# Graph network, layers 2 and 3: the vector and scalar engines follow one order written by hand instead of the scheduler's, and the edge bias is worked out in layer 1

## Chip, cores and metric

The kernel runs on one core of a Trainium2 chip. The metric is the device time of one execution in microseconds. Six engines appear in the profile: PE (matrix multiply) with PEld (its weight loads), DVE (vector), ACT (scalar), POOL (GpSimd) and SP (sync). In this kernel SP starts the plain DMA transfers, and POOL starts the indirect ones, the gathers and scatters by index.

## What is computed

Four graph layers follow one another on 3125 nodes with 128 features and 100,000 edges. Each layer's result is added to its input and normalized. Layer 0 is an attention with relation types, layer 1 a mean over neighbours with two matrix products, layer 2 an attention with 4 heads, layer 3 an attention with one head and a key matrix for each of 8 edge types. The change is in layers 2 and 3, and in a corner of layer 1:

```
# layer 2
Q, K, V = (x @ Wq, x @ Wk, x @ Wv)                  # 4 heads of 32
edge_bias = edge_attr @ We
attn = jnp.sum(Q[dst] * K[src], axis=-1) * SCALE + edge_bias
attn = jnp.where(attn >= 0, attn, 0.2 * attn)
attn_exp = jnp.exp(attn - jnp.max(attn))
attn_sum = jax.ops.segment_sum(attn_exp, dst, num_segments=n)
attn_norm = attn_exp / jnp.maximum(attn_sum[dst], 1e-12)
agg = jax.ops.segment_sum(V[src] * attn_norm[:, :, None], dst, num_segments=n)
h = jnp.concatenate([x, agg @ Wo + bo], axis=1) @ Wm + bm
return jax.nn.relu(h)

# layer 3
Q, K, V = (_type_matmul(x, W_Q, node_type), ...)
k_t = _type_matmul(K[src], W_edge, edge_type)
scores = jnp.sum(Q[dst] * k_t, axis=-1) / scale * mu[edge_type]
attn = _sparse_softmax(scores, dst, N)
out = jax.ops.segment_sum(V[src] * attn[:, None], dst, num_segments=N)
```

## The kernel before

The nodes are sorted by degree and cut into 25 tiles of 128, one node in each partition. `CAP[t]` is the number of edge slots that tile t has for each of its nodes: 57, 42, 40 and so on down to 21, together 821. Slots are handled in chunks of `W` = 8, so tile t has CAP[t]/8 chunks, rounded up; over all tiles there are 114. What exceeds the slots is taken by a loop (`behind`) that makes no trip with these inputs.

Layers 2 and 3 have the same shape. For each slot POOL issues one gather (`gather`, L103): 128 rows of 256 floats, keys in the first half and values in the second, from a table in DRAM (`kv_tab` in layer 2, `ktv_tab` in layer 3) into a chunk buffer `kv`. There are 8 such buffers in layer 2 and 12 in layer 3. A chunk then passes four long DVE instructions:

- `qk<-kv,qp` (L1220 in layer 2, L1378 in layer 3) multiplies the keys with the query of the node,
- `lg<-qk` (L1221, L1379) adds that up to one logit for each slot and head,
- `msg<-kv,ex` (L726, in `weigh`) multiplies the values with the softmax weights,
- `u<-msg` (L730) adds the weighted values over the slots, and `accb<-accb,u` (L731) adds `u` to the sum of the tile.

Between the second and the third stands a chain of short instructions for each group of chunks (in layer 2 a group is up to 3 chunks, from `segments`; in layer 3 all chunks of a tile): edge bias and leaky step in layer 2 (`biased`, L1226 to L1232), then in `weights` the maximum (L701), the new maximum `mn` (L703), `corr` (L705), the subtraction (L706), the exponentials on ACT (L707, L708), and the totals (L711 to L715). A tile in layer 2 ends with `closing` (matrix products on PE, a layer norm) and `table3`, which works out the tile's rows of `ktv_tab` on PE and ACT and has POOL scatter them (`put`, L106); a tile in layer 3 ends with a layer norm and a scatter of the output.

No order is written out: a scheduler places the instructions of all engines, and adds the semaphores. A buffer comes free when the last instruction that reads it is done; a gather into it waits for that on POOL, and everything behind it in POOL's queue waits too. In layer 2 the index of a gather comes from `pay_sb`, a 2463 KB array that SP loads at the start of layer 2 (L1201); it also holds the edge attributes of the bias.

Of the kernel before, what the change touches and what calls it, by code (L numbers as in the profile page):

```python
# [8 lines left out]
F32 = mybir.dt.float32  # L9
F16 = mybir.dt.float16  # L10
BF16 = mybir.dt.bfloat16
I32 = mybir.dt.int32
# [76 lines left out]
def tile_gnn(ctx, tc, a, out):  # L89
# [633 lines left out]
    def weigh(pool, acc, val, ex, n, heads):  # L723

        msg = pool.tile([P, W, D], F32, name="msg")
        V.tensor_tensor(msg[:, :n, :].rearrange("p s (h d) -> p s h d", h=heads),  # L726
                        val.rearrange("p s (h d) -> p s h d", h=heads),
                        ex.unsqueeze(3).to_broadcast([P, n, heads, D // heads]), op=OP.mult)
        u = pool.tile([P, D], F32, name="u", bufs=1)
        V.tensor_reduce(u, msg[:, :n, :].rearrange("p s d -> p d s"), AX.X, OP.add)  # L730
        V.tensor_add(acc, acc, u)  # L731

    def query(ps, q):

        qp = ps.tile([P, D], F32, name="qp", bufs=2)
        A.activation(qp, q, AF.Copy)
        return qp

# [329 lines left out]

    with ExitStack() as ctx1, tc.tile_pool(name="l1", bufs=2) as wp, tc.tile_pool(name="l1s", bufs=1) as sp:
# [90 lines left out]
        nc.sync.dma_start(xn, x1_tab.rearrange("(t p) d -> p t d", p=P))  # L1160
        for c in range(NCW):
# [30 lines left out]
    early.close()  # L1192


    H2 = 4
# [4 lines left out]
    pay_sb = big.tile([P, NS, PW], I32, name="pay_sb")  # L1200
    nc.sync.dma_start(pay_sb.rearrange("p s w -> p (s w)"), pay_tab)  # L1201
    with tc.tile_pool(name="l2", bufs=2) as wp, tc.tile_pool(name="l2s", bufs=1) as sp, \
            tc.tile_pool(name="l2p", bufs=1, space=PSUM) as ps1:

        we = row_of(sp, a["L2_gnn_We"].rearrange("k h -> (k h)"), 3 * H2, "we")
        weT = we.rearrange("p (k h) -> p h k", k=3)
        m = sp.tile([P, NT, H2], F32, name="m")
        V.memset(m, LOW)
# [6 lines left out]
        def rows2(qp, pl, n, lg):  # L1215
            kv = wp.tile([P, W, 2 * D], F32, name="kv", bufs=8)
            for s in range(n):
                gather(kv[:, s, :], kv_tab, pl[:, s, 0:1])
            qk = wp.tile([P, W, D], F32, name="qk")
            V.tensor_mul(qk[:, :n], kv[:, :n, :D], qp.unsqueeze(1).to_broadcast([P, n, D]))  # L1220
            V.tensor_reduce(lg, qk[:, :n].rearrange("p s (h d) -> p s h d", h=H2), AX.X, OP.add)  # L1221
            return kv

        def biased(pl, n, lg, mk):
            eb = wp.tile([P, 5 * W, H2, 3], F32, name="eb")
            V.tensor_tensor(eb[:, :n], pl.bitcast(F32)[:, :, 3:6].unsqueeze(2).to_broadcast([P, n, H2, 3]),  # L1226
                            weT.unsqueeze(1).to_broadcast([P, n, H2, 3]), op=OP.mult)
            bias = wp.tile([P, max(CAP), H2], F32, name="bias")
            V.tensor_reduce(bias[:, :n], eb[:, :n], AX.X, OP.add)
            V.scalar_tensor_tensor(lg, lg, (D // H2) ** -0.5, bias[:, :n], op0=OP.mult, op1=OP.add)  # L1230
            V.scalar_tensor_tensor(lg, lg, 0.2, lg, op0=OP.mult, op1=OP.max)
            V.tensor_add(lg, lg, mk.unsqueeze(2).to_broadcast([P, n, H2]))  # L1232

        def behind2(t, pl, mk, rl):
            lg = wp.tile([P, max(CAP), H2], F32, name="lg")
            kv = rows2(query(ps1, qb[:, t, :]), pl, W, lg[:, :W])
            biased(pl, W, lg[:, :W], mk)
            ex = ps1.tile([P, max(CAP), H2], F32, name="ex")
            corr = softmax(wp, lg[:, :W], W, H2, m[:, t, :], l[:, t, :], ex[:, :W])
            faded(accb[:, t, :], corr, H2)  # L1240
            weigh(wp, accb[:, t, :], kv[:, :, D:], ex[:, :W], W, H2)
# [21 lines left out]
        def closing(t, scale):  # L1263
# [13 lines left out]
            T.matmul(h_ps, oT, wm[:, 1, :], start=False, stop=True)  # L1277
            y = wp.tile([P, D], F32, name="y")
            V.tensor_add(y, h_ps, bm)
            V.scalar_tensor_tensor(y, y, 0.0, xb[:, t, :], op0=OP.max, op1=OP.add)  # L1280
            layernorm(wp, xb[:, t, :], y, t)

        def table3(t):


            of = wp.tile([P, NTY, P], F32, name="of", bufs=1)
            for k in range(NTY):
                V.tensor_scalar(of[:, k, :], ident, is_t[:, k, t:t + 1], None, op0=OP.mult)
            xk_ps = ps1.tile([P, NTY, P], F32, name="xk_ps", tag="dense")
            T.matmul(xk_ps, xb[:, t, :], of, start=True, stop=True)  # L1290
            xkT = wp.tile([P, NTY, P], F32, name="xkT", bufs=1)
            A.activation(xkT, xk_ps, AF.Copy)
            p_ps = ps1.tile([P, 3 * D], F32, name="p_ps")
            for k in range(NTY):
                T.matmul(p_ps, xkT[:, k, :], wqkv[:, k, :], start=(k == 0), stop=(k == NTY - 1))
            qkv = wp.tile([P, 3 * D], F32, name="qkv")
            A.activation(qkv, p_ps, AF.Copy)
            V.tensor_copy(qb[:, t, :], qkv[:, :D])
            kT = transposed(wp, ps1, qkv[:, D:2 * D], "kT")
            rows = wp.tile([P, NET, 2 * D], F32, name="rows")  # L1300
            for e0 in range(0, NET, 4):
                e_ps = ps1.tile([P, 4, D], F32, name="e_ps", bufs=2)
                T.matmul(e_ps, kT, wed[:, e0:e0 + 4, :], start=True, stop=True)
                V.tensor_mul(rows[:, e0:e0 + 4, :D], e_ps, mu[:, e0:e0 + 4].unsqueeze(2).to_broadcast([P, 4, D]))
            A.activation(rows[:, :, D:], qkv[:, 2 * D:].unsqueeze(1).to_broadcast([P, NET, D]), AF.Copy)
            put(ktv_tab, od, t, rows.rearrange("p e f -> p (e f)"))

        for t in range(NT):
            qp = query(ps1, qb[:, t, :])
            for s0, s1, run in segments(t):  # L1310
                lg = wp.tile([P, max(CAP), H2], F32, name="lg")
                parts = []
                for c0, w in run:
                    o = OFF[t] + c0
                    parts.append(rows2(qp, pay_sb[:, o:o + w], w, lg[:, c0 - s0:c0 - s0 + w]))
                n, o = s1 - s0, OFF[t] + s0
                biased(pay_sb[:, o:o + n], n, lg[:, :n], mask[:, o:o + n])
                ex = ps1.tile([P, max(CAP), H2], F32, name="ex")
                corr, rest = weights(wp, lg[:, :n], n, H2, m[:, t, :], l[:, t, :], ex[:, :n])
                faded(accb[:, t, :], corr, H2)  # L1320
                for (c0, w), kv in zip(run, parts):
                    weigh(wp, accb[:, t, :], kv[:, :w, D:], ex[:, c0 - s0:c0 - s0 + w], w, H2)
                rest()

            rl = wp.tile([P, H2], F32, name="rl")
            V.tensor_scalar(rl, l[:, t, :], 1e-12, None, op0=OP.max)
            V.reciprocal(rl, rl)
            closing(t, rl)
            table3(t)
# [111 lines left out]
```

## Time and profile before

| | us |
|---|---|
| median of 3 runs | 5285.81 (5254.62 to 5292.59) |
| profiled execution, its own time | 5243.0 |
| profiled execution, span from first to last instruction | 5241.3 |
| layer 0 and setup, to 2490 | 2490 |
| layer 1, to 2668 | 178 |
| gather of the tiles' own rows (25 gathers), to 2707 | 39 |
| layer 2, first to last kv gather, to 3928 | 1221 |
| from there to the first gather of layer 3, to 4010 | 82 |
| layer 3, first to last gather, to 5192 | 1182 |
| to the end | 49 |

The profile is of one execution. "busy" of an engine is the time in which it executes; "idle before" is the time just ahead of an instruction in which its engine did nothing, with what ended it. "issue" there means that the profile shows nothing that it waited for, and "remote" (in the chain: "another core or an unknown queue") that a semaphore event did whose source the profile doesn't know. For POOL, a gather's busy time is the time of its issue; the data lands later.

### The profile page before, as it was taken

To read this page: it belongs to the slowest core of one execution; us is meant where nothing else is said; L and a number is where in the kernel's file an instruction comes from. 1 tells how busy PE (TensorE), PEld (TensorE's weight loads), DVE (VectorE), ACT (ScalarE), POOL (GpSimd) and SP (SyncE) were. 2 spreads that over 40 slices of the span, in tenths; PEclk is the share of its full clock that TensorE was granted. 3 is DMA by queue.
4 is the path that set the end of the run, shared out by engine and by line. 5 is a ranking of instruction groups with operands and counts; after the bars stand their busy time and mean duration, and the time that the engine had idled before them with its cause. 6 is when DMAs were issued, how large, how long until landed. Compare 5 with 4: busy or idle time off the path is not lost. (4 is left out here: it accounts for less than half of the span.)

```text
span 5241.3 us, 41048 instructions
## 1 busy us (share of the span) xinstructions
PE 2170.7 (41%) x12091; PEld 1405.0 (27%) x12091; DVE 3025.1 (58%) x7369; ACT 1018.4 (19%) x2777; POOL 2860.7 (55%) x3030
## 2 busy tenths in 40 slices
PE   7267676677767677777830122222232000000000
PEld 5145444455545454545310001011111000000000
DVE  8346555666656666656224576556664554454646
ACT  1023233333333333332100111111111000000000
POOL 0545444555545454453047666666663777666664
PEclk9578778778877787878865555555566555555555
DMA  3423222333323233332533333333342333233232
GB/s 82 122 80 86 80 80 80 87 99 90 99 79 87 75 90 86 82 97 75 215 106 99 99 109 106 109 105 113 104 113 73 105 96 93 79 92 94 86 92 58
DMA packets 213060, 498.45 MB, mean 95 GB/s; under 512 B 62329, under 2 KB 109100, under 8 KB 208185
## 3 DMA queue, kind: packets, MB, share of 16 engines
q0 software_dynamic: 136448, 397.65, 26.8%
q1 hardware_dynamic: 76344, 97.76, 6.0%
q8 instruction: 102, 1.67, 0.1%
q14 instruction: 166, 1.36, 0.1%
HBM read 424.65 MB, written 70.63 MB: 94 GB/s over the span
## 5 line engine op out<-in xcount | busy, mean ns | idle before, releaser
L103 POOL DMA_INDIRECT kv<-kv_tab,pay_sb x821 | 783.2, 954 | 384.9 <-issue 245.6
L103 POOL DMA_INDIRECT hs<-h_tab,srcx x821 | 848.3, 1033 | 262.0 <-issue 212.9
L103 POOL DMA_INDIRECT kv<-ktv_tab,pay_sb x821 | 802.6, 978 | 333.0 <-issue 244.2
L730 DVE TENSOR_REDUCE u<-msg 128x128 f32<-128x1024 f32 (+4 forms) x228 | 384.0, 1684 | 144.4 <-remote 94.6
L892 PE MATMUL zps<-oh,zq 128*128 128x512 bf16 x1232 | 397.4, 443 | 37.1 <-DVE oh L883 20.7
L835 PE MATMUL lg<-yw,low 128*128 128x8 f32 x1642 | 242.0, 274 | 150.0 <-ACT low L831 72.7
L849 POOL COPY hs<-gates 1x8 f32<-1x8 f32 (+3 forms) x133 | 41.2, 310 | 467.0 <-ACT gates L833 446.6
L835 PEld LDWEIGHTS lg<-yw,low 128*128 128x128 f32 x1642 | 234.5, 218 | 210.3 <-ACT low L831 100.1
L103 POOL DMA_INDIRECT zs<-z_tab,rel x205 | 213.1, 1039 | 124.7 <-issue 55.2
L623 ACT ACTIVATE c_oha<-c_oha,srclo 128x50 bf16<-128x50 bf16 (+2 forms) x821 | 206.0, 345 | 264.9 <-DVE c_oha L571 193.0
L904 PE MATMUL t_ps<-zw,zT 128*128 128x136 f32 x1232 | 225.7, 312 | 75.2 <-DVE hs L905 36.4
L905 DVE TENSOR_TENSOR hs<-hs,t_ps 128x408 f32<-128x408 f32 (+1 forms) x231 | 122.0, 528 | 227.8 <-PE t_ps L904 81.3
L726 DVE TENSOR_TENSOR msg<-kv,ex 128x1024 f32<-128x1024 f32 (+4 forms) x228 | 248.7, 1102 | 2.9 <-issue 1.8
L896 PE MATMUL pre<-zT,zw 128*128 128x512 f32 x308 | 205.7, 756 | 101.6 <-issue 62.4
L741 PE MATMUL tp<-ident,an 128*128 128x128 f32 x25 | 11.3, 453 | 560.7 <-DMA kv<-kv_tab,pay_sb 172.0
L904 PEld LDWEIGHTS t_ps<-zw,zT 128*128 128x128 f32 x1232 | 194.5, 213 | 109.7 <-issue 50.0
L898 PEld LDWEIGHTS pre<-ident,hs 128*128 128x128 f32 x1232 | 189.0, 221 | 95.3 <-issue 94.6
L824 PE MATMUL pre<-identb,hq 128*128 128x512 bf16 (+3 forms) x645 | 204.6, 417 | 5.9 <-issue 3.4
L831 ACT ACTIVATE low<-pre 128x512 f32<-128x512 f32 (+2 forms) x215 | 122.9, 574 | 400.8 <-PE pre L898 159.1
L1290 PE MATMUL xk_ps<-of,xqb 128*128 128x512 f32 x50 | 50.9, 1121 | 358.0 <-DVE xqb L759 204.9
L898 PE MATMUL pre<-ident,hs 128*128 128x128 f32 x1232 | 194.1, 306 | 0.0
L1378 DVE TENSOR_TENSOR qk<-kv,qp 128x1024 f32<-128x1024 f32 (+4 forms) x114 | 126.5, 1110 | 114.9 <-DMA kv<-ktv_tab,pay_sb 98.2
(399 smaller groups left out, 5384.6 us busy)
## 6 DMA issues: line engine op xcount, KB each, us to landing
rb<-rel_tab SPq DMA_DIRECT2D x77, 256.0 KB
c_tab<-c_sb SPq DMA_DIRECT2D x25, 768.0 KB
cs<-c_tab SPq DMA_DIRECT2D x6, 3200.0 KB
hs<-h_tab,srcx POOLq DMA_INDIRECT x821
kv<-kv_tab,pay_sb POOLq DMA_INDIRECT x821
kv<-ktv_tab,pay_sb POOLq DMA_INDIRECT x821
h_tab<-h SPq DMA_DIRECT2D x25, 132.0 KB
zs<-z_tab,rel POOLq DMA_INDIRECT x205
```

The costliest lines, as they stand in the source:

```text
L103: return G.indirect_dma_start(out=dst, out_offset=None, in_=table, in_offset=indirect(idx), **kw)
L623: A.activation(oha[:, s // 2, 0, :, s % 2], oha[:, s // 2, 1, :, s % 2], AF.Copy, scale=srclo[:, o:o + 1])
L726: V.tensor_tensor(msg[:, :n, :].rearrange("p s (h d) -> p s h d", h=heads), val.rearrange("p s (h d) -> p s h d", h=heads), ex.unsqueeze(3 ...
L730: V.tensor_reduce(u, msg[:, :n, :].rearrange("p s d -> p d s"), AX.X, OP.add)
L824: T.matmul(pre[:, :k], hq[:, i, :], identb.unsqueeze(1).to_broadcast([P, k, P]), start=(i == 0), stop=False)
L831: A.activation(low[:, :k], pre[:, :k], AF.Relu)
L835: T.matmul(lg_ps[:, s, :], low[:, s, :], yw8, start=True, stop=True)
L892: T.matmul(zps, zq[:, i, 2 * R * k2:2 * R * (k2 + 1)], ohs[i][:, cols], start=(i + k2 == 0), stop=(i == NK - 1 and k2 == 1))
L896: T.matmul(pre[:, :k], zw[:, :D], zT[:, cols], start=False, stop=False)
L898: T.matmul(pre[:, s, :], hs[:, s0 + s, :D], ident, start=False, stop=(s == k - 1))
L904: T.matmul(t_ps[:, s, :], zT[:, (s0 + s) * P:(s0 + s + 1) * P], zw[:, D:], start=True, stop=True)
L1378: V.tensor_mul(qk[:, :n], kv[:, :n, :D], qp.unsqueeze(1).to_broadcast([P, n, D]))
```

## The change

It changes what DVE and ACT do in layers 2 and 3, and the order in which they do it. POOL's, PE's and SP's instructions stay with the scheduler. The instruction order of layer 0 is the same on every engine before and after.

- The long products work in place: keys are multiplied inside `kv`, and so are the values; `qk` and `msg` are gone. `kv` has 10 buffers in layer 2 (8 before) and 14 in layer 3 (12 before), and a buffer is free after the sum over its slots instead of after the multiplication.
- The query is scaled by a negative number when ACT copies it, so logits carry the other sign, maxima become minima, and the exponential takes them with `scale=-1`. In layer 3 ACT's exponential subtracts the maximum itself and adds up its results.
- The edge bias of all 821 slots and 4 heads is worked out once, in layer 1, from `pays` (the same 2463 KB array), with the mask of the empty slots in it: one copy and 12 instructions on 128x821. The load stands on SP's queue ahead of the first `cs` load (a 3200 KB piece of a count matrix that layer 1's products need). The gathers of layer 2 take their index from `srcx`, those of layer 3 from `idx3`.
- `passes` writes the order out, in beats of one chunk: multiply the keys of the new chunk, multiply the values of an older chunk, add up the new logits, add up the older values. Behind each of the four stands a slot, in which every lane (short chain of a group, totals, closing, table, scatter) may issue one step. `yield n` in a chain leaves n slots out. A scatter is traced 16 (layer 2) or 20 (layer 3) slots after its rows are.

In the built program a chunk of layer 2 is added up five beats after its keys are multiplied, one of layer 3 ten beats after, throughout.

```
+        with tc.tile_pool(name="l1pay", bufs=1) as pp:
+            pays = pp.tile([P, NS, PW], I32, name="pays")
+            nc.sync.dma_start(pays.rearrange("p s w -> p (s w)"), pay_tab)
+            V.tensor_copy(idx3, pays[:, :, 2])
+            for h in range(H2):
+                for k in range(3):
+                    V.scalar_tensor_tensor(bias[:, :, h], pays.bitcast(F32)[:, :, 3 + k],
+                                           we[:, k * H2 + h:k * H2 + h + 1], mask if k == 0 else bias[:, :, h],
+                                           op0=OP.mult, op1=OP.add)
...
-    pay_sb = big.tile([P, NS, PW], I32, name="pay_sb")
-    nc.sync.dma_start(pay_sb.rearrange("p s w -> p (s w)"), pay_tab)
...
+    def keyed(kv, qp, n):
+        k = kv[:, :n, :D]
+        V.tensor_mul(k, k, qp.unsqueeze(1).to_broadcast([P, n, D]))
+    def scored(kv, n, heads, lg):
+        V.tensor_reduce(lg, kv[:, :n, :D].rearrange("p s (h d) -> p s h d", h=heads), AX.X, OP.add)
+    def weighed(kv, n, heads, ex):
+        v = kv[:, :n, D:].rearrange("p s (h d) -> p s h d", h=heads)
+        V.tensor_tensor(v, v, ex.unsqueeze(3).to_broadcast([P, n, heads, D // heads]), op=OP.mult)
+    def summed(pool, kv, n):
+        u = pool.tile([P, D], F32, name="u", bufs=3)
+        V.tensor_reduce(u, kv[:, :n, D:].rearrange("p s d -> p d s"), AX.X, OP.add)
+        return u
...
+        def beat(key=None, score=None):
+            part = ready.pop(0) if ready else None
+            if key:
+                key()
+            lanes.slot()
+            if part:
+                g, kv, w, ex = part
+                first = g.left == len(g.run)
+                g.begun += 1
+                weighed(kv, w, heads, ex)
+                if first:
+                    faded_in(g)
+            lanes.slot()
+            if score:
+                score()
+                lanes.slot()
+            if part:
+                u = summed(pool, kv, w)
+                lanes.add("sum", add_up(g, u, first), 1)
+            lanes.slot()
+        for g in groups:
+            for c0, w in g.run:
+                kv, qp = rows(g, c0, w)
+                g.kvs.append(kv)
+                beat(lambda: keyed(kv, qp, w), lambda: scored(kv, w, heads, g.lg[:, c0 - g.s0:c0 - g.s0 + w]))
+            lanes.add("chain", chain(g, lanes, opened, older))
+        while lanes.busy() or ready:
+            beat()
...
+    LANES = ("sum", "chain", "total", "close", "table", "put")
+    ORDERED = {mybir.EngineType.DVE, mybir.EngineType.Activation}
...
+        def chain2(g, lanes, opened, older):
+            V.tensor_sub(lg, lg, bias[:, g.o:g.o + n])
+            yield 0
+            V.scalar_tensor_tensor(lg, lg, 0.2, lg, op0=OP.mult, op1=OP.min)
+            yield 0
+            mx = least(wp, lg, H2)
+            yield 0
+            V.tensor_tensor(mn, tops[t], mx, op=OP.min)
+            yield 0
+            V.tensor_sub(corr, mn, tops[t])
+            yield 0
+            while older(g):
+                yield 0
+            V.tensor_sub(lg, lg, mn.unsqueeze(1).to_broadcast([P, n, H2]))
+            A.activation(corr, corr, AF.Exp)
+            A.activation(ex, lg, AF.Exp, scale=-1.0)
+            yield 0
+            opened(g, ex)
...
+        def chain3(g, lanes, opened, older):
+            V.tensor_sub(lg, lg, mask[:, g.o:g.o + n])
+            yield 0
+            mx = least(wp, g.lg[:, :n], 1)
+            yield 0
+            V.tensor_tensor(mn, m[:, t, :], mx, op=OP.min)
+            yield 0
+            A.activation(ex[:, :, 0], lg, AF.Exp, scale=-1.0, bias=mn, accum_out=sm)
+            A.activation(corr, m[:, t, :], AF.Exp, scale=-1.0, bias=mn)
+            yield 0
+            opened(g, ex)
...
+        with tc.manual_schedule(engines=ORDERED):
+            passes(wp, H2, groups2(), main2, chain2, fade2, add2, finished2)
```

## The prediction

> **What bounds the kernel now.** I read the busy shares, then the table of windows cut at the stages' borders, then POOL's waits, then DVE's groups with the idle time before them, and the timeline where groups left a question.
>
> ```profile
> PE 2170.7 (41%) x12091; PEld 1405.0 (27%) x12091; DVE 3025.1 (58%) x7369; ACT 1018.4 (19%) x2777; POOL 2860.7 (55%) x3030
> ```
>
> No engine is busy for more than 58% over all, so the bound has to be looked for stage by stage. The columns below are the window, its length, and busy us (instructions) of PE, PEld, DVE, ACT and POOL; layer 2 from its first to its last gather, the way to layer 3, layer 3, the tail:
>
> ```profile
> 2707.00:3928.00 1221.00, 270.25 (x504) 121.70 (x505) 730.58 (x1563) 152.64 (x337) 803.80 (x842) 0.56 0.36 106
> 3928.00:4010.00 82.00, 33.63 (x76) 15.01 (x74) 49.97 (x123) 17.92 (x36) 4.08 (x5) 0.71 0.14 55
> 4010.00:5192.00 1182.00, 0.00 (x0) 0.00 (x0) 605.44 (x937) 48.82 (x114) 824.07 (x842) 0.50 0.32 92
> 5192.00:5241.30 49.30, 0.00 (x0) 0.00 (x0) 41.46 (x86) 3.74 (x9) 3.99 (x4) 0.50 0.03 7
> ```
>
> In both layers POOL is the busiest, DVE next with half of the window idle, DMA at a third. POOL's timeline shows what 842 indirect DMAs cost at best:
>
> ```profile
> 4123.13 0.95 POOL L103 DMA_INDIRECT kv<-ktv_tab,pay_sb  x1 [0.30 <-issue]
> 4124.39 0.95 POOL L103 DMA_INDIRECT kv<-ktv_tab,pay_sb  x1 [0.30 <-issue]
> ```
>
> One per 1.255 us: 0.95 busy, and 0.30 that waits for nothing. So 842 need 842 x 1.255 = 1057 us. Layer 2 takes 1221, that is 164 more, layer 3 takes 1182, that is 125 more. Of the latter some 20 are no waits: between 4245 and 4514 the gathers last 1.09 or 1.79 instead of 0.95 us with nothing ahead of them. The rest are waits, in layer 2
>
> ```profile
> POOL kv L103 <- DVE msg L726: 53.2, 8, 17.3
> POOL kv L103 <- DVE bn_sd L752: 33.5, 4, 10.2
> POOL kv L103 <- DVE bn_mv L750: 29.3, 4, 9.5
> POOL kv L103 <- DVE bn_st L748: 12.6, 2, 9.5
> ```
>
> (total, times, longest), besides scatters of `ktv_tab` that wait for DVE, ACT and the rows. All stand ahead of gathers in one queue: POOL stops until DVE has read a buffer or a tile's chain is through. DVE is late although it is idle for 490 us of layer 2's window, only 57 of them for data. Why, shows in its groups of layer 3 (count | busy, mean ns | idle before, by what ended it):
>
> ```profile
> L730 DVE TENSOR_REDUCE u<-msg 128x128 f32<-128x1024 f32 x92 | 171.8, 1867 | 84.0 <-remote 61.8 <-DVE msg L726 9.9 <-issue 8.6
> L1378 DVE TENSOR_TENSOR qk<-kv,qp 128x1024 f32<-128x1024 f32 x92 | 112.0, 1218 | 114.4 <-DMA kv<-ktv_tab,pay_sb 98.2 <-issue 15.2
> L1379 DVE TENSOR_REDUCE lg<-qk 128x8 f32<-128x1024 f32 x92 | 111.5, 1212 | 27.7 <-issue 12.8 <-DVE mx L701 4.8 <-remote 3.6
> ```
>
> Only 98 us of idle end with data. `u`, which reads what the instruction ahead of it wrote, has 84 us of idle before it: 0.9 us each. The timeline shows that as it happens:
>
> ```profile
> 4683.81 0.29 DVE L731 TENSOR_TENSOR accb<-accb,u 128x128 f32<-128x128 f32 x1
> 4685.21 0.16 DVE L715 TENSOR_TENSOR l<-l,sm 128x1 f32<-128x1 f32 x1 [1.11 <-DVE accb L731]
> ...
> 4690.11 0.29 DVE L731 TENSOR_TENSOR accb<-accb,u 128x128 f32<-128x128 f32 x1 [2.45 <-remote]
> 4691.51 0.17 DVE L1415 RECIPROCAL rcl<-rcl 128x1 f32<-128x1 f32 x1 [1.11 <-DVE accb L731]
> ```
>
> 0.29 us of work, then 1.11 us of nothing before the next; starts lie 1.40 us apart, in both places. Where the producer stands two or more instructions back, the next starts at once (`lg` at 4725.57, `accb` at 4726.70). There are also stretches (3220 to 3260) where neighbours follow each other without a gap, while POOL gathers at full rate: the price of a self-wait is not constant.
>
> **The change, part by part, against the span of 5241.3.**
>
> *Bias in layer 1.* The load of 2463 KB now stands ahead of `cs` on SP's queue. The stage that loads `cs` (2506 to 2522) moves 406 GB/s, so 2.46 MB hold everything behind by 6 us. The 13 instructions on 128x821 are not in the trace; `msg` moves 1024 elements per partition in 1.21 us, so 821 contiguous ones need about 1 us, with a stride perhaps 1.5: 12 to 18 us on DVE, ahead of the first `hT` there. They lie beside the first tile's matmuls (2519.4 to 2537.2). Uncovered they would cost up to 12. I take +6 in all: 2668 becomes 2674. In layer 2 the load of `pay_sb` and its DMA go, and so does the short bias work of 47 groups, per group `eb` and `bias` (0.35 to 0.45 each) and the masks' share of three times 0.22: some 56 us of DVE. POOL is the bound there, so I count these as cover, not as gain. The gathers of the tiles' own rows take 39 as before: 2713.
>
> *Layer 2.* Per chunk DVE has 1.14 (`qk`) + 1.13 (`lg`) + 1.13 (`msg`) + 1.79 (`u`) + 0.2 (`accb`, behind `u`'s pipeline) + some 1.9 for its share of the short steps, layer norm and table: 7.1 us, against 8 x 1.255 = 10.0 of POOL for its gathers. In the written order long instructions of two chunks alternate and each slot takes one step of each lane, so hardly any instruction waits on the one just ahead; the 1.1 to 4 us gaps then have nothing to start from. A buffer is held until its sum, five beats after its keys: of ten buffers about four are then ahead of DVE, or 40 us of POOL. The longest single wait of DVE in the whole trace is 5.0 us, and a tile's waits on PE and ACT (`h_ps`, `qkv`, the two `e_ps`, the root of the layer norm, the `exp`) are some six: 28 + 6 x 5.0 = 58 us of DVE against 42 of POOL in a small tile, if all were longest; at 1.5 each, 37. So POOL paces, with a little left over: 842 x 1.255 = 1057, plus 15 for the first fill and rare waits: 1072. The first scatter of `ktv_tab` now follows 178 gathers instead of 139 and its rows 16 slots back, so its wait should go too. Against 1221 that is -149.
>
> *To layer 3.* Now 82 us: the last tile's closing and table until 3996, and 14 until the first gather. The drain is five beats of some 3.6 us (two long instructions), then one closing and table of the same matmuls, but one scatter more stands behind the last gather. 72 taken (-10), 62 to 90 possible.
>
> *Layer 3.* 5.8 us of DVE per chunk, 10 beats of lag, 14 buffers, so three ahead (30 us). 1057 + 20 for the long gathers, which nothing here removes, + 10 residual = 1087, -95.
>
> *Tail.* Ten draining beats at 3.4 us, 6.5 for the chain and 10 for the last output: 51 (+2), 45 to 60 possible.
>
> *`u` in place.* It now reads values at a stride of 1024 instead of 512 bytes. No row has that; contiguous `lg` takes 1.18 ns per element, strided `u` 1.82. If the longer stride doubled it to 3.6 us, layer 3's beat would be 7.6, still under 10.0: no cost to the end. It would need 5 us to be felt in layer 2.
>
> Sum: 6 - 149 - 10 - 95 + 2 = -246; the profiled execution would span 4995. That execution (5243.0) lies 43 below the median of the runs, which would give 5040 for a median; I take 5025, between the two, nearer the median because that is what is measured.
>
> **A rule that speaks against it.** The row is the 84.0 us of idle before 92 `u`, each behind its producer. The Trainium skill ("VectorE: DVE Perf Modes", section "The DRAIN you can't avoid") says that a semaphore after each of eight copies takes as long as one after the last, 13.88 us, so a wait on the instruction ahead costs nothing. By the rule the order removes no gap that is DVE's own: it would keep those that come from pipeline and short instructions, some 430 us of layer 2's 490 and 479 of layer 3's 577 (all but the data). With 56 us of bias gone, DVE would need 700 + 430 = 1130 in layer 2 and 617 + 479 = 1096 in layer 3, or -91 and -86, to near 5110. The timeline contradicts the rule in slow stretches (1.11 us of nothing after 0.29 us) and agrees with it in the others, so I go by the row, and let the rule hold the upper part of the range.
>
> **Rivals.**
> - *A, POOL's issue is all that is left:* 5025. For it: 1.255 us in stretch after stretch, DVE with 30% to spare. Chance 0.70.
> - *B, about half of the stalls stay:* because the gaps are not of self-waits only, or because DVE and POOL slow each other whatever the order. Half of 246 gone: 5286 - 123 = 5163; with the rule, 5110. For it: `remote` ends most of `u`'s idle, a source that I do not know. Chance 0.19.
> - *C, it doesn't do what it says:* gathers run at 1.40 us as in 4245 to 4514, throughout, because a steadily fed DVE slows POOL's issue. 842 x 0.145 = 122 more per layer: 5025 + 244 = 5269, no change. For it: those 270 us exist; against it: in 3220 to 3260 DVE is gapless and POOL at 1.255. Chance 0.05.
> - *D, slower:* one fixed order lets a late PE or ACT result hold all DVE work behind it, keys and sums with it, so no buffer comes free. A tile of layer 2 has 28 us of DVE work and six such waits; with w us each, 25 x (28 + 6w) passes the 1318 that would eat the gain of both layers (1072 + 246) at w = 4.1. At 5.0, the longest seen, layer 2 takes 1450, +229 on its 1221: 5286 + 229 - 95 - 2 = 5418. Against it: chains leave slots out (`yield n`) so that results are there. Chance 0.06.
>
> **Numbers.** Likeliest 5025. A measurement of this kernel can tell about 1% from no change (5233 to 5339). A and B are faster: 0.89; C the same: 0.05; D slower: 0.06. The range holds A with its bounds (30 us off the residuals and boundary, and the 43 of the median: down to 4955) and the rule's 5110 and most of B (up to 5150); C and D lie outside.
>
> **What the profile after would show.** Gathers of layer 2 in about 1072 us and of layer 3 in about 1087; POOL's waits for `kv` on DVE near zero, "issue" unchanged near 245 us per layer; idle before `u` and `accb` gone, and DVE's idle ending mostly in data of `kv`; the own-row gathers starting about 6 us later; bias beside layer 1's first matmuls. It would be wrong if the gathers' mean rose over 1.0 us (C), if DVE showed long waits on PE and ACT (D), or gaps before instructions whose producer is two back (B).

## The result, and the profile after

| | before | changed |
|---|---|---|
| median of 20 runs, us | 5280.38 (5248.22 to 5301.61) | 5252.55 (5216.74 to 5289.01) |
| ratio, 95% interval | | 0.9948 [0.9926, 0.9969] |
| forecast | | 5025 (4955 to 5150) |

The kernel became faster by half a per cent instead of five. The chips on which the runs of this study fell are of two kinds, and that has to be known to read any of them: on some (called held here) the kernel before takes 5213 to 5302 us, as in the first measurement, on others (called free) 4381 to 4396. No chip of the experiments was measured on two occasions, so whether the kind belongs to the chip or to the occasion is open. A second pair of traces on another held chip (r_before and r_after: 5237.2 and 5214.11 us, ratio 0.9958 [0.9935, 0.9981]) repeats the first, so the stages stand side by side:

| stage, us | before | changed | forecast | before, 2nd | changed, 2nd |
|---|---|---|---|---|---|
| until the first load that layer 1's stage begins with | 2507.0 | 2511.0 | | 2497.2 | 2469.7 |
| from there to the first own-row gather | 161.1 | 169.0 | +6 | 162.7 | 168.1 |
| own-row gathers | 39.2 | 39.2 | 0 | 38.9 | 38.9 |
| layer 2, first to last gather | 1221 | 1194 | 1072 | 1220 | 1191 |
| way to layer 3 | 82 | 104 | 72 | 96 | 95 |
| layer 3 | 1182 | 1151 | 1087 | 1172 | 1151 |
| tail | 49 | 65 | 51 | 65 | 65 |

Both pairs agree on the first row that the change touches (+8 and +5) and on the two layers (-27 and -31, -29 and -21). The way between the layers and the tail moved in the first pair and not in the second; layer 0, whose instructions did not change, moved by +4 and -27. So the change does -44 to -50 in layer 1 and the two layers, while the medians moved by only -28 and -23. Part of the rest is lost on the way between the layers: in all traces from held chips it takes 82 to 96 us before (three traces) and 95 to 104 in those with the changed order (seven), where -10 was forecast.

The windows of the changed kernel (first pair: layer 2, the way, layer 3, tail; behind the five engines stand the granted clock, the busy share of the DMA engines, and GB/s):

```profile
2719.20:3912.70 1193.50, 241.80 (x469) 107.96 (x469) 666.82 (x1333) 145.42 (x322) 800.70 (x841) 0.57 0.36 108
3912.70:4016.30 103.60, 45.64 (x110) 20.90 (x110) 59.31 (x140) 23.63 (x49) 5.01 (x5) 0.75 0.14 54
4016.30:5167.50 1151.20, 0.00 (x0) 0.00 (x0) 564.29 (x776) 78.60 (x154) 871.28 (x841) 0.50 0.33 95
5167.50:5232.50 65.00, 0.00 (x0) 0.00 (x0) 42.44 (x71) 7.49 (x14) 4.97 (x5) 0.50 0.02 7
```

DVE has fewer instructions (1333 for 1563, 776 for 937) and less to do (667 for 731 us, 564 for 605). POOL's busy time is the same in layer 2 and 47 us longer in layer 3. Where POOL waits in layer 2:

```profile
POOL kv L103 <- DVE y L1428: 54.4, 12, 10.4
POOL kv L103 <- remote: 26.6, 7, 5.7
POOL kv L103 <- DVE an L1412: 20.9, 4, 7.1
POOL kv L103 <- DVE kv L1206: 15.5, 4, 7.9
```

POOL's waits, most of them for DVE, are there as before, on other names: 31 of them, 136 us, where there were 21 with 161 (waits over 0.6 us, counted beyond the usual 0.30). In layer 3 they are gone, and the groups of DVE look as they were to look (`u` and the sum of logits have no idle time, the key product waits for data):

```profile
L1217 DVE TENSOR_REDUCE u<-kv 128x128 f32<-128x1024 f32 x83 | 154.4, 1861 | 0.0
L1206 DVE TENSOR_TENSOR kv<-kv,qp 128x1024 f32<-128x1024 f32 x92 | 112.3, 1221 | 522.8 <-DMA kv<-ktv_tab,idx 458.4 <-issue 64.4
L1209 DVE TENSOR_REDUCE lg<-kv 128x8 f32<-128x1024 f32 x91 | 110.2, 1211 | 2.1 <-DVE kv L1213 1.9
```

And yet the layer is 94 us longer than 842 x 1.255. POOL's timeline shows the gathers themselves:

```profile
4267.28 0.99 POOL L103 DMA_INDIRECT kv<-ktv_tab,idx  x1 [0.30 <-issue]
4268.58 1.09 POOL L103 DMA_INDIRECT kv<-ktv_tab,idx  x1 [0.30 <-issue]
4269.98 1.09 POOL L103 DMA_INDIRECT kv<-ktv_tab,idx  x1 [0.30 <-issue]
4271.38 0.95 POOL L103 DMA_INDIRECT kv<-ktv_tab,idx  x1 [0.30 <-issue]
```

From 4244 on, after 182 of 842, gathers start 1.40 us apart in the mean (many still 1.25, others 1.40 to 2.10), though hardly any wait is recorded; they do so to the end of the layer. DVE in layer 2 shows the same spacing, and at instructions whose producers have long ended:

```profile
2965.61 1.22 DVE L1213 TENSOR_TENSOR kv<-kv,ex 128x1024 f32<-128x1024 f32 x1
2966.74 0.25 DVE L1491 TENSOR_TENSOR lg<-lg,ml 128x96 f32<-128x96 f32 x1
2969.03 1.22 DVE L1209 TENSOR_REDUCE lg<-kv 128x32 f32<-128x1024 f32 x1 [2.04 <-issue]
2970.47 0.29 DVE L1426 TENSOR_TENSOR y<-h_ps,bm 128x128 f32<-128x128 f32 x1 [0.22 <-PE h_ps L1423]
2972.53 1.87 DVE L1217 TENSOR_REDUCE u<-kv 128x128 f32<-128x1024 f32 x1 [1.77 <-remote]
```

`u` at 2972.53 needs the weighting of L1213, which had ended at 2966.8, and three other instructions stand in between; it starts 5.7 us later. 2969.03 to 2972.53 is 3.50 us, five times 0.70. That is no wait on the instruction just ahead, and it is what the experiments had to explain.

### The profile page after: what moved, and what is told of

It is laid out like the page before. It is cut to its first block, busy times and chain, and to the rows that moved or that the text cites. A ratio compares the mean times of both kernels' runs of the same rounds, so it can differ in the third digit from the quotient of the medians.

```text
span 5232.5 us, 40540 instructions
## 1 busy us (share of the span) xinstructions
PE 2147.6 (41%) x11947; PEld 1403.6 (27%) x12091; DVE 2950.1 (56%) x6986; ACT 1050.2 (20%) x2820; POOL 2912.1 (56%) x3030
## 5 line engine op out<-in xcount | busy, mean ns | idle before, releaser
L103 POOL DMA_INDIRECT kv<-ktv_tab,idx x821 | 850.5, 1036 | 288.4 <-issue 283.1
L103 POOL DMA_INDIRECT kv<-kv_tab,srcx x821 | 780.9, 951 | 393.2 <-issue 246.5
L1206 DVE TENSOR_TENSOR kv<-kv,qp 128x1024 f32<-128x1024 f32 (+4 forms) x228 | 252.9, 1109 | 657.8 <-DMA kv<-ktv_tab,idx 482.9
L1217 DVE TENSOR_REDUCE u<-kv 128x128 f32<-128x1024 f32 (+4 forms) x228 | 383.0, 1680 | 24.5 <-remote 10.8
L876 PE MATMUL zps<-oh,zq 128*128 128x512 bf16 x1100 | 362.0, 443 | 39.0 <-DVE oh L867 22.6
L1209 DVE TENSOR_REDUCE lg<-kv 128x32 f32<-128x1024 f32 (+5 forms) x228 | 251.4, 1103 | 9.5 <-issue 4.6
L1213 DVE TENSOR_TENSOR kv<-kv,ex 128x1024 f32<-128x1024 f32 (+4 forms) x228 | 252.0, 1105 | 0.0
L649 PE MATMUL c_ps<-c_ohs,c_ohd 128*128 128x128 bf16 x1300 | 134.0, 252 | 163.7 <-ACT c_sb L651 89.6
```

The costliest lines, as they stand in the source:

```text
L103: return G.indirect_dma_start(out=dst, out_offset=None, in_=table, in_offset=indirect(idx), **kw)
L876: T.matmul(zps, zq[:, i, 2 * R * k2:2 * R * (k2 + 1)], ohs[i][:, cols], start=(i + k2 == 0), stop=(i == NK - 1 and k2 == 1))
L1206: V.tensor_mul(k, k, qp.unsqueeze(1).to_broadcast([P, n, D]))
L1209: V.tensor_reduce(lg, kv[:, :n, :D].rearrange("p s (h d) -> p s h d", h=heads), AX.X, OP.add)
L1213: V.tensor_tensor(v, v, ex.unsqueeze(3).to_broadcast([P, n, heads, D // heads]), op=OP.mult)
L1217: V.tensor_reduce(u, kv[:, :n, D:].rearrange("p s d -> p d s"), AX.X, OP.add)
```

## The experiments

The theories as they stood: **W**, DVE's gaps come from waits on the instruction just ahead (the prediction); **O**, the order is what brings the gain; **C**, a busy DVE lengthens POOL's gathers; **S**, each engine's instructions come at a limited rate once a reserve is used up, whatever they wait for; **F**, S because straight-line code is delivered too slowly; **P**, the engines themselves are slower.

**The first four fell on a free chip** (the kernel before: 4388.0 us). *The pinned order taken away:*

```
-        with tc.manual_schedule(engines=ORDERED):
+        if True:
```

> The changed kernel with the written order taken away in layers 2 and 3 (the scheduler places DVE and ACT again); products in place, buffers, signs and the bias in layer 1 stay. If the order is what brought the 28 us of layer 2 and the 31 us of layer 3 (theory O), both stages go back to 1221 and 1182 or more, and the time to that of before or above it. If the two stages are set by a rate at which DVE and POOL get their instructions, whatever the order (theory S), both stages stay within 30 us of the changed kernel's 1193 and 1151.

4394.19 us, ratio to before 1.0012 [1.0006, 1.0019]. *Eight short instructions more per beat in layer 3:*

```
+    def pulse(k):
+        for i in range(2):
+            V.memset(pulses[0][:, 2 * k + i:2 * k + i + 1], 0.0)
...
             lanes.slot()
+            pulse(0)
```

> The changed kernel with eight independent memsets of one element per partition in every beat of layer 3, two behind each of the four slots; they wait for nothing near them. They are 8 x 124 x some 0.06 us = 60 us of DVE work, where DVE is idle for 587 of 1151 us. Theory W (gaps come from waits on the instruction just ahead): layer 3 stays at 1151 within 15 us. Theory S (DVE's instructions come at a limited rate): 15.3 instead of 7.3 instructions per chunk, and layer 2, which is short of DVE, sustains 1.12 per us; 124 beats x 15.3 / 1.12 = some 1700 us at that rate, in any case over 1300, with POOL waiting for DVE.

4409.31 us (one run). *Layer 3 without values:*

```
-                weighed(kv, w, heads, ex)
+                if heads > 1:
+                    weighed(kv, w, heads, ex)
...
-                u = summed(pool, kv, w)
+                u = summed(pool, kv, w) if heads > 1 else None
```

> The changed kernel; layer 3 leaves out the multiplication of the values, their sum and the addition to accb (three of about seven DVE instructions of a chunk), so its output there is not the layer's. POOL's gathers are the same. Theory C (a busier DVE makes POOL's gathers longer): they stay at 0.95 us throughout, layer 3 takes about 1060. Theory S (POOL's own instructions come at a limited rate once a reserve is used up): they go over to 1.40 us per gather after about 180, as in the changed kernel, and layer 3 stays near 1150.

4375.82 us. *Pauses for POOL:*

```
             kv = wp.tile([P, W, 2 * D], F32, name="kv", bufs=14)
+            for _ in range(rest):
+                nc.gpsimd.memset(kv, 0.0)
```

> The changed kernel; at the start of tiles 4, 9, 14 and 19 of layer 3 POOL first fills the tile's first chunk buffer with zeros five times (some 2 us each, so four pauses of about 10 us without gathers). Nothing else waits for that. Theory S: each pause lets POOL's reserve fill up, the gathers go back to 0.95 us for some 200 to 400 gathers, and layer 3 takes 1057 + 40 + up to 40 = 1100 to 1140 although 40 us of work were added. Without such a reserve the pauses come on top: 1190.

4442.69 us, 1.0128 [1.0111, 1.0145]: the pauses come on top, 38 us in layer 3 (1091 for 1053). On this chip no theory could be told from another, because nothing was late. The windows of e1_scheduled, layers 2 and 3:

```profile
2169.00:3225.50 1056.50, 244.12 (x491) 108.81 (x491) 675.92 (x1362) 153.84 (x335) 800.17 (x841) 0.58 0.41 122
3293.50:4349.00 1055.50, 0.00 (x0) 0.00 (x0) 564.43 (x779) 80.37 (x158) 799.11 (x842) 0.50 0.36 103
```

Both layers are 842 x 1.255 = 1057 within 2 us, with eight more instructions per beat as well (1055 in layer 3). Since all of this kernel takes 4394 and the one before 4388, the two layers of the latter cannot lie much over 1057 either: on a free chip there was nothing to gain. (That is worked out from the times; no trace of the kernel before was had there.)

**Three on a held chip.** The kernel before and the changed one, and *the load behind layer 1's loop* (the block with `pays` moved from ahead of the loop to behind it):

> The kernel before, unchanged, to have its trace on the chip of these runs: in the first four runs it took 4388 us, 900 less than where the change was measured, and no gather of them waited or was long. Theory S' (where instructions come without delay, POOL's 1.255 us per indirect DMA is all that bounds layers 2 and 3 already before the change): both stages take 1057 to 1085 us, DVE shows no starts on a grid of 0.70 us, and the waits of POOL for DVE are under 30 us per layer. Theory W (self-waits of DVE hold POOL on every chip): the stages stay over 1130.

> The changed kernel, unchanged, beside the one before. Theory S': the two stages at 1057 to 1065 us like the first four runs, so no more than 25 us per layer can be gained, against some 9 us lost in layer 1, and 10 to 20 at the end of layer 3: within 0.5% of before, either sign. Theory W: 100 us or more faster than before.

> The changed kernel; the load of the 2463 KB and the 13 bias instructions stand behind layer 1's loop instead of ahead of its first load. If the load ahead of cs cost layer 1 some 9 us, the first gather of layer 2 comes 6 to 9 us earlier against the start of layer 1 and the time falls by as much; if the load is hidden anyway, nothing changes.

The stages are in the table above; S' and W both spoke of a free chip. e5_late_pays took 5218.91 us, 0.9958 [0.9934, 0.9982], the same as the changed kernel: the first `hT` came 29.9 us after the first load instead of 35.9, but the first own-row gather after 168.3 instead of 168.1. Later in the layer the transfer costs about as much. The forecast of +6 for the transfer holds. Whether it can be hidden is not shown: in the trace of this run SP starts the load 1.3 us after the first `cs` load, as the third load of the layer, and the second tile's `hT` comes after 57.7 us, where r_before has 52.4. The edit moved it behind two loads, not behind the loop.

**Four on another held chip** (the kernel before: 5232.02 us), the kernels of e1 to e4:

> The kernel of e1_scheduled once more, for a chip like the one of r_before and r_after, where layers 2 and 3 take 1220 and 1172 us before and 1191 and 1151 after. Theory O (the written order brings the gain): about 1220 and 1170, the time that of before. Theory S (each engine gets its instructions at a limited rate there; the order is worth little, the number of instructions is what counts, and this kernel has as few as the changed one): 1191 and 1151 within 20 us. On a chip like the one of the first four runs: 1057 each again.

> The kernel of e2_extra_dve (eight independent one-element memsets more per beat of layer 3) for a chip like that of r_after. Theory S: layer 3 over 1300 us, DVE idle before instructions that wait for nothing, POOL waiting for DVE and its gathers back at 0.95 us. Theory W (only waits on the instruction just ahead are slow): 1151 within 20 us.

> The kernel of e3_light (no weighting and no sum of the values in layer 3, which is left out of the output) for a chip like that of r_after. Theory C (a busy DVE lengthens POOL's gathers): gathers at 0.95 us, layer 3 near 1060. Theory S with a rate for each engine of its own: gathers at 1.40 us apart from about the 180th on, layer 3 near 1150. If the engines share one rate: between the two.

> The kernel of e4_pause (four pauses of POOL in layer 3; on the chip of the first four runs they took 13 us each) for a chip like that of r_after. Theory S with a reserve that fills in a pause: the mean of a gather falls from 1.04 to under 0.98 us, and layer 3 takes 1100 to 1150 in spite of 50 us of pauses. No reserve: 1200.

| run | layer 2 | layer 3 | gathers of layer 3, mean | POOL's waits over 0.6 us in layer 3 | DVE instructions in layer 3 |
|---|---|---|---|---|---|
| r_before | 1220 | 1172 | 0.977 | 11, 87 us | 913 |
| r_after | 1191 | 1151 | 1.033 | none | 776 |
| s1_scheduled | 1195 | 1151 | 1.039 | none | 776 |
| s2_extra_dve | 1190 | 1182 | 0.948 | 34, 127 us | 1654 |
| s3_light | 1193 | 1151 | 1.035 | 2, 2 us | 472 |
| s4_pause | 1185 | 1156 | 0.947 | 31, 46 us | 764 |

The group of layer 3's gathers (count | busy, mean ns | idle before) in s2_extra_dve has the mean of 0.95 us, with 54 us of idle time ended by DVE and 60 by a source that the profile doesn't name:

```profile
L103 POOL DMA_INDIRECT kv<-ktv_tab,idx x821 | 778.1, 948 | 373.9 <-issue 251.9 <-remote 60.2 <-DVE kv L1206 53.7
```

In s3_light it has no such waits, and a mean of 1.035:

```profile
L103 POOL DMA_INDIRECT kv<-ktv_tab,idx x821 | 849.5, 1035 | 289.2 <-issue 289.2
```

In s4_pause the mean is back at 0.947, though not the pace:

```profile
L103 POOL DMA_INDIRECT kv<-ktv_tab,idx x821 | 777.2, 947 | 309.9 <-issue 302.5 <-remote 5.3 <-DVE kv L1213 1.5
```

s3 settles C: with about half of DVE's work gone the gathers are as long as before (1035 ns) and the layer as long, 1151. s2 goes against W: instructions that wait for nothing lengthen the layer by 31 us and bring POOL's waits back, the gathers at 0.95 us. But S had expected over 1300; 1182 is well short of that, so one fixed rate for all instructions was wrong too. s4: four pauses that cost 38 us on the free chip leave the layer at 1156 instead of 1189, just above the 1150 that S expected. After a pause gathers start 1.25 us apart again, for 80 us or more; then they slip back towards 1.40, and here the delay stands between them and not in their own length. Of the 46 us of waits in the table five with a cause have 24; the others are this spacing. s1 (5202.69 us, 0.9948 [0.9928, 0.9967], the same as the changed kernel) says less about O than hoped: of 2311 DVE rows from layer 2 on, 2193 stand in the order of the changed kernel. It shows that pinning the order is worth nothing, not what the order is worth. On the free chips the pinning even costs on the way between the layers: 79 and 80 us (m2_blocks, m1_blocks) after 68 without it (e1_scheduled).

**The rate by itself.** Behind the changed kernel, after its output, three blocks: `ca` is block A (`NM` is 400), `cb` block B, which begins when gather 40 of 450 has landed, and the loop is block C (`pull` is one gather):

```
+            for i in range(1, NM):
+                V.memset(ca[:, i:i + 1], 0.0)
...
+            V.tensor_copy(cb[:, :1], tr[39 % 8][:, :1])
+            for i in range(1, NM):
+                V.memset(cb[:, i:i + 1], 0.0)
...
+        with tc.For_i(0, 8, 1):
+            for i in range(50):
+                pull(i)
+            for i in range(50):
+                V.memset(cc[:, i:i + 1], 0.0)
```

> The changed kernel with three blocks behind it, after its output is written; they measure how fast DVE gets through instructions that wait for nothing. Block A: 400 memsets of one element in a row, no transfers. Block B: 400 more, while POOL issues 450 gathers of 128 KB in a row. Block C: a loop of 8 trips, each with 50 gathers and 50 memsets. Theory F (straight-line code is delivered too slowly on this kind of chip while gathers run): A goes at under 0.2 us per memset, B at 0.7 to 1.4 us once a reserve of some tens is used up and its gathers pass over to 1.40 us after about 180, C at under 0.2 us from the second trip on, because the loop's code is there already, with gathers at 1.25. Theory P (the engines themselves are slower there): A, B and C at one pace. On a chip like that of the first four runs all three go at under 0.2 us.

> The kernel of m1_blocks once more, for a chip like that of r_after; where it ran first, a memset took under 0.1 us and a gather 1.25 us in all three blocks, and no layer lost time. Theory F (straight-line code comes too slowly there while gathers run): block A under 0.2 us per memset after the first, B 0.7 to 1.4 us per memset and gathers passing over to 1.40 us, C under 0.2 us and 1.25 us from the second trip on. Theory P (the engines are slower there): A, B and C at one pace, slower than 0.1 us.

> The kernel of m1_blocks a third time, still for a chip like that of r_after; on two other chips a memset took 0.06 us and a gather 1.25 us in all three blocks. Theory F: block A under 0.2 us per memset, B 0.7 to 1.4 us per memset and gathers passing over to 1.40 us, C under 0.2 us and 1.25 us from the second trip on. Theory P: A, B and C at one pace, slower than 0.1 us. On a chip like that of the first four runs: as before, and then the run beside it shows the kernel before there.

m1 and m2 fell on free chips (5521.38 and 5516.01 us), m3 on a held one (6444.48). DVE's groups for the three blocks on the free chip of m2_blocks:

```profile
L1723 DVE MEMSET cc<- 128x1 f32 x400 | 11.5, 59 | 963.2 <-PEq L1719 962.8 <-issue 0.4
L1709 DVE MEMSET ca<- 128x1 f32 x399 | 11.3, 59 | 1.0 <-issue 1.0
L1716 DVE MEMSET cb<- 128x1 f32 x399 | 11.3, 59 | 1.0 <-issue 1.0
```

And on the held chip of m3_blocks:

```profile
L1716 DVE MEMSET cb<- 128x1 f32 x399 | 22.9, 59 | 507.7 <-issue 507.7
L1723 DVE MEMSET cc<- 128x1 f32 x400 | 19.4, 59 | 543.7 <-issue 332.5 <-PEq L1719 211.1
...
L1709 DVE MEMSET ca<- 128x1 f32 x399 | 11.3, 59 | 1.0 <-issue 1.0
```

Without transfers the held chip is as quick as the free one: A has 1.0 us of idle time in 400. With gathers beside it, B is idle for 508 us that nothing accounts for. The timeline of m3_blocks, where B begins on DVE:

```profile
5304.55 0.59 DVE L1716 MEMSET cb<- 128x1 f32 x21
5306.53 0.06 DVE L1716 MEMSET cb<- 128x1 f32 x1 [1.40 <-issue]
5308.63 0.06 DVE L1716 MEMSET cb<- 128x1 f32 x1 [2.04 <-issue]
5310.03 0.06 DVE L1716 MEMSET cb<- 128x1 f32 x1 [1.34 <-issue]
```

And on POOL about the 182nd gather of the block:

```profile
5479.15 0.98 POOL L103 DMA_INDIRECT tr<-kv_tab,srcx  x1 [0.30 <-issue]
5480.44 1.09 POOL L103 DMA_INDIRECT tr<-kv_tab,srcx  x1 [0.31 <-issue]
5481.84 1.10 POOL L103 DMA_INDIRECT tr<-kv_tab,srcx  x1 [0.30 <-issue]
5483.24 1.09 POOL L103 DMA_INDIRECT tr<-kv_tab,srcx  x1 [0.30 <-issue]
```

21 memsets go at once, and the other 378 take 530 us, 1.40 us each, although each needs 0.06 and waits for nothing. POOL's gathers keep 1.25 us for the first 182 and then go at 1.40 in the mean. One reading fits the blocks, and POOL in layer 3: for DVE and for POOL there is room for some 20 instructions each, and while gathers run it empties by one every 1.40 us. An engine faster than that fills it, and is then held to 1.40. POOL gains on it by 1/1.2535 - 1/1.40 = 0.083 instructions per us; over the 228 us of its first 182 gathers that is 19.

For DVE in the layers this reading is not enough. Two windows of s2_extra_dve's layer 3, the first just behind a stop of POOL of 6.45 us, the second soon after it:

```profile
4505.70:4531.30 25.60, 0.00 (x0) 0.00 (x0) 25.08 (x74) 2.64 (x4) 19.26 (x21) 0.50 0.33 95
4533.20:4554.20 21.00, 0.00 (x0) 0.00 (x0) 6.94 (x17) 1.58 (x2) 15.42 (x17) 0.50 0.35 102
```

In the first DVE gets through 74 instructions without a pause, where 20 + 25.6/1.40 = 38 would have been let through; in the second it is held to one per 1.24 us. POOL gathers close to its best pace in both. Layer 2 has such stretches too (up to 56 DVE instructions in 28 us). So a stop of POOL lifts the limit on DVE for some 25 us, in the layers; in the loop of block C, where gathers stop for about 10 us between trips, it does not. The law of the limit stays open.

P falls with A. F falls with C: in every trip of the loop but the first, which starts with DVE still held, about 21 memsets go at once and the rest at 1.40, with the code the same as in the trip before. Nor is the loop's code fetched anew. The DMA queues from 5305 to 5836 (block B) hold six packets of instructions, those from 5760 to 6420 (the loop) none (packets, MB, share):

```profile
q14 instruction: 6, 0.05, 0.0%
...
q0 software_dynamic: 22438, 61.29, 32.0%
```

The Trainium skill's page "Runtime: NRT & Kernel Launch" ("Instruction fetch mechanics") has the fetching of code mostly hidden, and the trace agrees: two such packets come in during block A, which has 1.0 us of idle time in all. Two other rivals fall by rows shown above: slower transfers (layer 3's share of the DMA engines is 0.36 of 1055.5 us on the free chip and 0.33 of 1151.2 on the held one, 380 us each) and the clock (0.50 granted in layer 3 on both).

**Not answered.** x1_short_chain and x3_short_chain (188 short instructions of layer 2 left out), and x2_light_pause (s3 and s4 together), fell on free chips. There they took 4398.63, 4398.99 and 4407.91 us, with layers 2 and 3 at 1053 to 1054 (layer 3 1087 with pauses), and say nothing about a held one. r_before2 was to show the kernel before on a free chip and fell on a held one: 5283.99 us, layers 1219 and 1174.

> The changed kernel; layer 2 leaves out the edge bias with its mask, the leaky step, the scaling of the totals and of the accumulator (four short instructions of each of 47 groups, 188 of some 1340, 42 us of DVE's busy time), so its output is not the layer's. Theory S (the number of instructions counts): POOL's waits of some 140 us in layer 2 fall by a third or more, the stage goes from 1191 to 1150 or less. Theory D (waits for PE and ACT hold DVE, rival D of the prediction): those stay, so the stage stays within 15 us of 1191. On a chip like that of the first four runs: 1057.

> s3_light and s4_pause together: layer 3 without weighting and sum of the values (left out of the output), and with four pauses of POOL of 13 us. Theory S: DVE no longer holds POOL, the pauses fill POOL's reserve, gathers at 0.95 us: layer 3 at 1057 + 52 = 1110, against 1151 without pauses. If pauses do not fill a reserve: 1151 + 52 = 1203.

> The kernel of x1_short_chain (188 short instructions of layer 2 left out of some 1340) for a chip like that of r_after. Theory S (the number of instructions counts): layer 2 goes from 1191 to 1150 or less. Theory D (waits for PE and ACT): within 15 us of 1191.

> The kernel before, unchanged, once more. On a chip like that of the first four runs theory S' expects layers 2 and 3 at 1057 to 1085 us already before the change, with under 30 us of waits of POOL for DVE in each, since its time there (4383 to 4388) is that of the changed kernel without the order (4394). On a chip like that of r_before: 1220 and 1172 again.

## Why the prediction was wrong

- **What bounds the kernel.** Right as far as it went: POOL's issue and its waits for DVE. On free chips 1.255 us per gather is all there is: the changed kernel took 1054 and 1053 us for the two layers of m1_blocks, close to the 1072 and 1087 of the forecast. The forecast was made from a trace of a held chip, and there the floor is another.
- **The failing step** is the one in layer 2's part: "the 1.1 to 4 us gaps then have nothing to start from". They need no wait to start from: on the held chips memsets that wait for nothing stand 1.40 us apart (block B), and 878 more instructions of that kind in layer 3 bring 127 us of waits to POOL (s2). The gaps come from a limit on how many instructions DVE gets through, and the change takes only 15% of the instructions away in layer 2 and 17% in layer 3. By the reading with 20 and 1.40 us, DVE has 1057/1.40 + 20 = 775 instructions per layer before it holds POOL at its best pace; that is an estimate, and the windows above show stretches with more. It fits layer 3 changed, which has 776, and POOL never waits for DVE over 0.6 us (before: 933 instructions, 95 us of waits). Layer 2 has 1333 after 1563, both far over it, and POOL waits 136 us after 161. The waits don't scale with the count (0.14 to 0.6 us per instruction above 775 in these runs), and that fewer instructions would shorten layer 2 no run on a held chip shows. Of the 149 us forecast for layer 2, 27 came.
- **The floor of layer 3** was the second mis-sized term: 1057 + 30 was put for 1151. The 20 us for "long gathers, which nothing here removes" were read as an episode; they are the pace into which POOL fell in each held trace of the changed kernel once nothing had stopped it for about 182 gathers. (842 - 20) x 1.40 = 1151 is what the layer took in r_after, s1 and s3. The waits for DVE before the change had kept POOL out of it: taking them away (87 to 95 us) gave back 64 to 66 in gathers further apart and left 21 to 31.
- **Rival C** had this: gathers at 1.40 us, 5269 in all, close to the 5252.55 measured. Its cause was wrong (a steadily fed DVE; s3 shows that it isn't), its price of 122 per layer was 94 in layer 3, and in layer 2 the gathers stayed at 0.95 us and DVE's waits at 136. It was dismissed on 40 us of the trace (3220 to 3260) that came right after a stop of POOL of 9.96 us (to 3214), the kind of stretch in which neither engine is held. The prediction's own signs for it and for B came: the mean of layer 3's gathers rose to 1.036 us, and gaps stand in layer 2 before instructions whose producer is not just ahead (2972.53).
- **The rule that spoke against the change** (the Trainium skill, "VectorE: DVE Perf Modes", "The DRAIN you can't avoid") was weighed the wrong way. On the free chips a wait on the instruction ahead costs nothing, as the page has it (in m2_blocks the leaky step at 2194.59 starts 0.03 us after the `lg` that it reads), and on the held ones the gaps come without such a wait. The row of 84.0 us before `u` was read by what the profile named as releaser; 61.8 of it said `remote`, a source that the prediction admitted not to know. The 1.40 us between starts stood in the prediction for two engines, in its lines for DVE and in rival C for POOL.
- **Rival D** (waits on PE and ACT) is not what holds layer 2: in m1_blocks the same order with the same PE and ACT work lets POOL go through in 1054 us. That was on a free chip; on a held one x1 and x3 were to tell, and didn't.
- **Right:** +6 for the load (+5 to +8), the bias beside the matmuls, `u` at its wider stride (1861 ns after 1867), and DVE's lighter work in layer 2 (64 us, 56 forecast). **Way and tail** (-10 and +2): +22 and +16 in one pair, 0 and 0 in the other; the traces together speak for a loss on the way. In the tail of both DVE was still held for some 25 us after the last gather.
- **Slips in its working,** none of which decides: the parts of DVE's 7.1 us per chunk add up to 7.3; 5.0 us is not DVE's longest wait, even with those for data left out (5.40 in layer 2 at 2884.8, 6.75 on the way at 3991.8); and 731 - 56 leaves DVE 675 in layer 2 where the rule's sum has 700.
- How much of the 27 and 31 us comes from fewer instructions, how much from their order and how much from the two more buffers in each layer is not separated. That more instructions, in the same order, bring layer 3 back to 1182 (s2) speaks for the count.

## What to carry to other kernels

Before a gap is put down to the wait in front of it, look at instructions that have no such wait, and at the spacing of starts: equal spacing before instructions that wait for nothing is a rate, not a dependency. Where an engine that sets the pace is freed of its waits, ask what it does when it never stops; here 21 to 31 of 87 to 95 us were left. Count instructions per stage as well as their time; on a held chip a memset of 0.06 us took up to 1.40. That taking instructions away wins this back is not shown.

## What the runs showed of the hardware that was not expected

The same program (the kernel before) took 4383 to 4388 us in the median on three chips and 5232 to 5286 where the others were measured. On the latter DVE passes one instruction per 1.40 us in blocks B and C, on a grid of 0.70, once it is some 20 ahead and gathers of 128 KB follow each other; POOL's gathers pass over to 1.40 in the mean after about 182 without a stop. For about 25 us after the last gather DVE stayed held (5167 to 5194), and with no transfers 400 instructions go in a row without it. It is no fixed rate: after a stop of POOL 74 instructions went in 25.6 us.

What the limit is, and the 20 and the 1.40 us, is open. Most of the difference between the two kinds of chips lies elsewhere: up to layer 1's first load a held chip takes 2511 us (the changed kernel) and a free one 1961 (e1_scheduled), with the same instructions, and there DVE starts 915 in 500 us (1000 to 1500), more than one per 1.40. No run looked into that part. Each run lists the span and clock of its core, so it carries the profiler's records, and no run shows whether an execution without them would be held as well.
